# A Mamba scan over image tokens: the last token's decay is multiplied by C on GpSimd, the first token's u is replicated by TensorE, and the whole order is rewritten

## The chip, the cores and the metric

The kernel runs on one NeuronCore of a Trainium2 chip. The metric is the device time of one execution in microseconds (us), the median of several runs. The engines named below are TensorE (PE, with PEld for its weight loads), VectorE (DVE), ScalarE (ACT), GpSimd (POOL), and SyncE (SP), which here only issues DMAs.

## The reference, cut to what matters

Four layers run one after the other on an image of shape (2, 128, 128, 128), that is batch, channels, rows, columns. Layers 0 and 2 are alike and are the subject. Layer 1 is a window gate, and layer 3 a block of two 3x3 convolutions with batch norm. In layers 0 and 2, a 3x3 convolution is followed by a small Mamba model that sees the 128 values of each pixel as 8 tokens of 16 features:

```python
y = conv3x3(x, conv_w) + conv_b
seq = y.reshape(B*H*W, 8, 16)                 # 8 tokens of 16
xi, z = split(seq @ in_proj_w.T)              # 32 each
xc = silu(causal_conv_over_tokens(xi) + conv1d_b)
dt, Bm, Cm = split(xc @ x_proj_w.T, [1, 17])  # 1, 16, 16
dt = softplus(dt @ dt_proj_w.T + dt_proj_b)   # 32
dA  = exp(dt[..., None] * A)                  # 32 x 16
dBx = dt[..., None] * Bm[:, :, None, :] * xc[..., None]
for t in range(8):
    h = dA[t] * h + dBx[t]                    # 32 x 16 states, h = 0 at first
    ys[t] = sum(h * Cm[t], axis=-1)
out = ((ys + D * xc) * silu(z)) @ out_proj_w.T
```

Then come a group norm, a silu and the residual, which other parts of the kernel do.

## The kernel before, in words

**Tiles.** `_mamba` works on tiles of 4 image rows, that is 512 pixels in the free dimension. There are 64 tiles in each of the two layers, 128 in all. The 32 x 16 states of one token of one tile are an array of 128 partitions by 4 x 512 elements (`NJ = 4`, `NS = 512`), all in fp32.

**One token.** For token t, `decay` (L460, L469) makes the decay: 4 matmuls with 32 rows each fill two PSUM buffers named `set` (1024 elements each, one for each half `jp`), and ACT takes the exponential in place. `token` (L478, L479, L483) then does three DVE operations for each half: the decay times the old state, into PSUM; this product times C, into `r`; and the product plus the injected term, into the new state `h`. The part of y that comes from the token's own injection is not in `r`. It is computed apart as (sum of B C) times u, in `product`, `own` and `own_u`, with u = dt * xc. So y of token t needs only decay * old state * C here, and the last token needs no new state, so it has two operations for each half in place of three. `gather` (L498) sums `r` over the 16 states on PE, into a PSUM buffer `ys`.

**The injected term.** `store` writes u, and B with C, to DRAM. `load` (L441 to L446) reads them back for each of the tokens 0 to 6, replicated over the partitions: 1 MB into `ur` and 0.5 MB into `bcr` for each token. `inject` (L451) multiplies the two on GpSimd into `h`.

**Before the scan.** For each tile `conv` (9 taps), `turn` (a transpose), `project` (4), `silu`, `inout` (B, then C), `step` (dt, 2), `softplus`, `product`, `scaled` (u), `own` (2) and `own_u` prepare the inputs. Every one of the 12 matmul groups among them writes to the single PSUM buffer `one`, and the next group waits until ACT has copied it out. After the scan `through`, `gate`, `out`, `spread` and `keep` finish the tile.

**PSUM.** Three `set` buffers of two banks, one `ys` and one `one` fill the eight banks.

**The order.** Nothing is scheduled automatically. Each piece of work of tile k gets a place, k * `SPAN` + a constant, as in

```python
put(k, REP_AT + t, decay, t)
...
for _, _, f, args in sorted(todo, key=lambda x: x[:2]):
    f(*args)
```

All pieces of all tiles are emitted in the order of their places, and each engine runs its own instructions strictly in that order. A place isn't a time. It only says what is queued behind what. Pieces of three or four tiles are interleaved: while tile k is in its scan, tile k+1 is stored and loaded, and tile k+2 is projected. A buffer is handed out at the place of its tile's first writer, and that writer waits until the last reader of the earlier tile in this buffer is done.

Of the kernel before, what the change touches and what calls it, by code (L numbers as in the profile page):

```python
# [24 lines left out]
F32 = mybir.dt.float32  # L25
U8 = mybir.dt.uint8
AF = mybir.ActivationFunctionType
ALU = mybir.AluOpType
# [3 lines left out]
P = 128  # L32
NT, FT = 8, 16
DI, DS, DC = 32, 16, 4
NQ = 4
NJ = DI * DS // P
DJ = DI // NJ
# [4 lines left out]
NS = ROWS * P  # L42
# [229 lines left out]

SPAN = NT - 1
BAND_AT = -22.0
CONV_AT = (-12.75, -12.7, -11.6, -11.5, -11.35, -11.25, -11.2, -11.05, -10.85)
TURN_AT = -10.5
IN_AT = (-10.0, -9.75, -9.65, -9.05)
SILU_AT = -8.52  # L280
BC_AT = (-8.25, -7.45)
DT_AT = (-7.85, -6.7)
SOFTPLUS_AT = -5.62
PROD_AT = -6.85
OWN_AT = (-6.3, -5.8)
U_AT, OWN_U_AT = -5.0, -4.3
STORE_AT = -4.15
LOAD_AT, INJECT_AT = -3.7, -1.8
REP_AT = -1.2
SUM_AT = 0.35  # L290
D_AT = (1.25, 4.2)
V_AT = (3.79, 7.39)
OUT_AT, STATS_AT, KEEP_AT = 7.9, 12.5, 13.85


def _mamba(tc, src, w, con, dst, scratch, stats, H):


    nc = tc.nc
    ctx = ExitStack()  # L300
    bandp = ctx.enter_context(tc.tile_pool(name="bandp", bufs=2))
    seq = ctx.enter_context(tc.tile_pool(name="seq", bufs=2))
    tmp = ctx.enter_context(tc.tile_pool(name="tmp", bufs=2))
    st = ctx.enter_context(tc.tile_pool(name="st", bufs=1))
    ps_set = ctx.enter_context(tc.tile_pool(name="ps_set", bufs=3, space=PSUM))
# [5 lines left out]
    live = {}  # L311
    bands = {}

    def one():
        return ps_one.tile([P, NS], F32, tag="one", name="one")
# [5 lines left out]
    def conv(k, tap):  # L321

        if tap == 0:
            live[k] = {"py": one(), "band": bands[k * ROWS // BAND]}
        xb, py = live[k]["band"], live[k]["py"]
        r = (k * ROWS) % BAND
        kh, kw = divmod(tap, 3)
        nc.tensor.matmul(  # L328
            py.rearrange("p (r w) -> p r w", r=ROWS),
            lhsT=w["conv"][:, tap, :],  # L330
            rhs=xb[:, r + kh : r + kh + ROWS, kw : kw + P],
            start=(tap == 0),
            stop=(tap == 8),
        )
        if tap == 8:
            yc = live[k]["yc"] = tmp.tile([P, NS], F32, tag="yc", name="yc")
            nc.scalar.activation(yc, py, AF.Identity, bias=w["conv_b"])

    def turn(k):

        s = live[k]
        p = one()
        for r in range(ROWS):
            nc.tensor.transpose(p[:, r * P : (r + 1) * P], s["yc"][:, r * P : (r + 1) * P], con["ident"])
        s["y"] = tmp.tile([P, NS], F32, tag="y", name="y")
        nc.scalar.copy(s["y"], p)

    def project(k, i, g):
# [16 lines left out]
    def step(k, g):  # L365
        s = live[k]
        if g == 0:
            s["dt"] = seq.tile([P, 2, NS], F32, tag="dt", name="dt")
        p = one()
        nc.tensor.matmul(p, lhsT=w["dt"], rhs=s["xc"][:, g, :], start=True, stop=True)  # L370
        nc.scalar.activation(s["dt"][:, g, :], p, AF.Identity, bias=w["dt_b"])
# [10 lines left out]
    def store(k):  # L382

        s = live[k]
        su = s["su"] = scratch.tile([NT, DJ, NJ, NS], F32, tag="su", name="su")
        for g in range(2):
            for j in range(NJ):
                nc.sync.dma_start(
                    out=su[g * NQ : (g + 1) * NQ, :, j, :].rearrange("q e s -> (q e) s"),
                    in_=s["u"][j * NQ * DJ : (j + 1) * NQ * DJ, g, :],  # L390
                )

        sb = s["sb"] = scratch.tile([NT - 1, DS, 2, NS], F32, tag="sb", name="sb")
        for i, at in enumerate((0, DS)):
            nc.sync.dma_start(
                out=sb[:, :, i].rearrange("t n s -> (t n) s"), in_=s["bc"][at : at + P - DS, i, :]
            )
# [16 lines left out]

    def product(k):
        s = live[k]
        s["prod"] = tmp.tile([P, NS], F32, tag="prod", name="prod")
        nc.gpsimd.tensor_tensor(s["prod"], s["bc"][:, 0, :], s["bc"][:, 1, :], ALU.mult)  # L418

    def own(k, g):  # L420
# [8 lines left out]
    def own_u(k):  # L429
# [2 lines left out]
        nc.scalar.activation(s["xc"], s["xc"], AF.Copy, scale=w["d"])  # L432
        nc.gpsimd.tensor_tensor(s["t1"], s["t1"], s["xc"], ALU.add)

    def load(k, t):

        s = live[k]
        n = P - DS
        ur = s["ur", t] = st.tile([P, NJ, NS], F32, tag="ur", name="ur", bufs=3)
        u = s["su"][t]  # L440
        nc.sync.dma_start(out=ur[:n], in_=u[: DJ - 1].unsqueeze(0).to_broadcast([DS, DJ - 1, NJ, NS]))  # L441
        nc.sync.dma_start(out=ur[n:], in_=u[DJ - 1].unsqueeze(0).to_broadcast([DS, NJ, NS]))
        m = s["bc", t] = st.tile([P, 2, NS], F32, tag="bcr", name="bcr", bufs=5)
        b = s["sb"][t]
        nc.sync.dma_start(out=m[:n], in_=b.unsqueeze(1).to_broadcast([DS, DJ - 1, 2, NS]))
        nc.sync.dma_start(out=m[n:], in_=b)  # L446
# [6 lines left out]
    def decay(k, t):  # L453

        s = live[k]
        g, q = divmod(t, NQ)
        a = s["a", t] = [ps_set.tile([P, 2, NS], F32, tag="set", name="set") for _ in range(2)]
        for j in range(NJ):
            r = slice(j * NQ * DJ, (j + 1) * NQ * DJ)
            nc.tensor.matmul(  # L460
                a[j // 2][:, j % 2, :],
                lhsT=w["rep"][r, q, :],
                rhs=s["dt"][r, g, :],
                start=True,
                stop=True,
                tile_position=(r.start, 0),
            )
        for x in a:
            nc.scalar.activation(x, x, AF.Exp)  # L469

    def token(k, t, jp):

        s = live[k]
        if jp == 0:
            s["r", t] = st.tile([P, NJ, NS], F32, tag="r", name="r", bufs=2)
        pt = s["a", t][jp]
        js = slice(2 * jp, 2 * jp + 2)
        nc.vector.tensor_tensor(pt, pt, s["h", t - 1][:, js, :], ALU.mult)  # L478
        nc.vector.tensor_tensor(  # L479
            s["r", t][:, js, :], pt, s["bc", t - 1][:, 1].unsqueeze(1).to_broadcast([P, 2, NS]), ALU.mult  # L480
        )
        if t < NT - 1:
            nc.vector.tensor_tensor(s["h", t][:, js, :], pt, s["h", t][:, js, :], ALU.add)  # L483

    def through(k, g):

# [52 lines left out]
    def put(k, at, f, *args):  # L539
        todo.append((k * SPAN + at, len(todo), f, (k, *args)))  # L540

    for k in range(len(src) * ntile):
        if k * ROWS % BAND == 0:
            put(k, BAND_AT, band)
        for tap in range(9):
            put(k, CONV_AT[tap], conv, tap)
        put(k, TURN_AT, turn)
        for n in range(4):
            put(k, IN_AT[n], project, *divmod(n, 2))
        put(k, SILU_AT, silu)  # L550
        for i in range(2):
            put(k, BC_AT[i], inout, i)
        for g in range(2):
            put(k, DT_AT[g], step, g)
        put(k, SOFTPLUS_AT, softplus)
        put(k, PROD_AT, product)
        put(k, U_AT, scaled)
        for g in range(2):
            put(k, OWN_AT[g], own, g)
        put(k, OWN_U_AT, own_u)  # L560
        put(k, STORE_AT, store)
        for t in range(NT - 1):
            put(k, LOAD_AT + t, load, t)
            put(k, INJECT_AT + t, inject, t)
        for t in range(1, NT):
            put(k, REP_AT + t, decay, t)
            for jp in range(2):
                put(k, t - 1 + jp / 2, token, t, jp)
            put(k, SUM_AT + t, gather, t)
        for g in range(2):  # L570
            put(k, D_AT[g], through, g)
            put(k, V_AT[g], gate, g)
        put(k, OUT_AT, out)
        put(k, STATS_AT, spread)
        put(k, KEEP_AT, keep)
# [420 lines left out]
```

## Time and profile before

The median of 3 runs is 7862.33 us (7861.02 to 7884.91). The profiled execution has a span of 7860.9 us.

| | PE | DVE | ACT | POOL |
|---|---|---|---|---|
| busy us in the whole span | 6537.9 | 6831.1 | 4291.8 | 5521.1 |
| busy us in 600 us inside the first scan layer (1000 to 1600) | 510.7 | 574.3 | 363.8 | 473.8 |

A row of the profile's groups gives the line, the engine, the operation, output and input, the shapes and the count, then the busy time and the mean of one in ns, then the idle time of the engine just before these instructions and what ended it. In the timeline a row has the start and the duration in us, and in brackets the wait just before it with what ended it. "x8" on a PE row counts instructions: an fp32 matmul of 512 columns shows as two of them, so a convolution tap is x2 and one `decay` or `gather` is x8.

### The profile page before, as it was taken

To read this page: it belongs to the slowest core of one execution; us is meant where nothing else is said; L and a number is where in the kernel's file an instruction comes from. 1 tells how busy PE (TensorE), PEld (TensorE's weight loads), DVE (VectorE), ACT (ScalarE), POOL (GpSimd) and SP (SyncE) were. 2 spreads that over 40 slices of the span, in tenths; PEclk is the share of its full clock that TensorE was granted. 3 is DMA by queue.
4 is the path that set the end of the run, shared out by engine and by line. 5 is a ranking of instruction groups with operands and counts; after the bars stand their busy time and mean duration, and the time that the engine had idled before them with its cause. 6 is when DMAs were issued, how large, how long until landed. Compare 5 with 4: busy or idle time off the path is not lost. (4 is left out here: it accounts for less than half of the span.)

```text
span 7860.9 us, 86792 instructions
## 1 busy us (share of the span) xinstructions
PE 6537.9 (83%) x29412; PEld 2217.4 (28%) x29412; DVE 6831.1 (87%) x6360; ACT 4291.8 (55%) x4835; POOL 5521.1 (70%) x1810
## 2 busy tenths in 40 slices
PE   7888888888888888777888888888888888878893
PEld 2222222222222222253222222222222222223341
DVE  5999999999999999863999999999999999963454
ACT  5656666666666656482665665666656656621112
POOL 5777887777778777652777778787777777843330
PEclk8999999999999999866999999999999999979996
DMA  7999999999999999854999999999999999955204
GB/s 203 246 243 246 253 249 247 253 250 256 249 248 254 245 249 248 225 179 127 244 249 246 250 250 251 252 251 253 252 239 249 250 250 250 250 157 139 69 0 163
DMA packets 573435, 1765.42 MB, mean 225 GB/s; under 512 B 85536, under 2 KB 239680, under 8 KB 458176
## 3 DMA queue, kind: packets, MB, share of 16 engines
q1 hardware_dynamic: 530496, 1709.54, 84.0%
q10 hardware_dynamic: 42496, 50.34, 1.8%
q8 instruction: 234, 3.83, 0.2%
q14 instruction: 209, 1.71, 0.1%
HBM read 1549.82 MB, written 209.72 MB: 224 GB/s over the span
## 5 line engine op out<-in xcount | busy, mean ns | idle before, releaser
L451 POOL TENSOR_TENSOR h<-ur,bcr 128x2048 f32<-128x2048 f32 x896 | 4060.4, 4539 | 1193.2 <-DMA bcr<-sb 1006.0
L478 DVE TENSOR_TENSOR set<-set,h 128x1024 f32<-128x1024 f32 x1792 | 2193.0, 1224 | 301.6 <-ACT set L469 216.2
L479 DVE TENSOR_TENSOR r<-set,bcr 128x1024 f32<-128x1024 f32 x1792 | 2194.1, 1224 | 61.4
L469 ACT ACTIVATE set<-set 128x1024 f32<-128x1024 f32 x1792 | 1745.6, 1006 | 868.7 <-PE set L460 854.2
L483 DVE TENSOR_TENSOR h<-set,h 128x1024 f32<-128x1024 f32 x1536 | 1864.5, 1214 | 21.3 <-POOL h L451 21.2
L460 PE MATMUL set<-dt,rep 32*128 32x512 f32 x7168 | 1400.2, 674 | 96.8 <-DVE h L483 89.9
L498 PE MATMUL ys<-r,ct 128*32 128x512 f32 x7168 | 1166.1, 632 | 36.4 <-DVE r L479 36.0
L328 PE MATMUL one<-band,conv 128*128 128x512 f32 x2304 | 1085.5, 607 | 24.6 <-DMA band<-in_x_dram 12.2
L828 PE MATMUL m<-comb,u 128*128 128x512 f32 x1536 | 689.1, 610 | 88.5 <-DVE Y L842 53.2
L406 PE MATMUL one<-xc,keep 128*64 128x512 f32 x1024 | 324.6, 717 | 471.4 <-ACT xc L363 361.5
L460 PEld LDWEIGHTS set<-dt,rep 32*128 32x128 f32 x7168 | 405.2, 193 | 992.7 <-issue 466.2
L328 PEld LDWEIGHTS one<-band,conv 128*128 128x128 f32 x2304 | 408.2, 190 | 674.4 <-issue 599.2
L489 PE MATMUL ys<-t,ct 128*128 128x512 f32 x512 | 326.4, 724 | 252.4 <-DVE v L511 250.9
L357 ACT ACTIVATE xc<-one,keep 128x512 f32<-128x512 f32 x256 | 176.1, 688 | 519.5 <-PE one L355 514.7
L498 PEld LDWEIGHTS ys<-r,ct 128*32 128x32 f32 x7168 | 181.2, 111 | 928.5 <-issue 760.7
L828 PEld LDWEIGHTS m<-comb,u 128*128 128x128 f32 x1536 | 296.6, 195 | 480.3 <-issue 457.3
L426 PE MATMUL one<-prod,ct 128*128 128x512 f32 x512 | 290.3, 650 | 123.1 <-POOL prod L418 88.8
L380 POOL TENSOR_TENSOR u<-dt,xc 128x1024 f32<-128x1024 f32 x128 | 302.8, 2366 | 70.7 <-ACT dt L374 70.6
L355 PE MATMUL one<-y,w_in 128*128 128x512 f32 x512 | 343.5, 759 | 5.8 <-ACT xc L357 3.1
L469 ACT ACT_TABLE_LOAD x252 | 323.3, 1283 | 4.6
L370 PE MATMUL one<-xc,w_dt 128*128 128x512 f32 x512 | 313.5, 696 | 4.1 <-ACT bc L413 4.1
L427 ACT COPY t<-one 128x512 f32<-128x512 f32 x256 | 150.2, 587 | 301.4 <-PE one L426 301.4
(136 smaller groups left out, 5894.0 us busy)
## 6 DMA issues: line engine op xcount, KB each, us to landing
ur<-su SPq DMA_DIRECT2D x896, 896.0 KB, 11.5
bcr<-sb SPq DMA_DIRECT2D x896, 448.0 KB, 11.6
ur<-su SPq DMA_DIRECT2D x896, 128.0 KB, 11.1
su<-u SPq DMA_DIRECT2D x1024, 64.0 KB, 3.5
sb<-bc SPq DMA_DIRECT2D x256, 224.0 KB, 2.8
bcr<-sb SPq DMA_DIRECT2D x896, 64.0 KB, 10.9
y<-o SPq DMA_DIRECT2D x128, 256.0 KB, 9.2
band<-in_x_dram SPq DMA_DIRECT2D x28, 640.0 KB, 10.9
```

The costliest lines, as they stand in the source:

```text
L328: nc.tensor.matmul(py.rearrange("p (r w) -> p r w", r=ROWS), lhsT=w["conv"][:, tap, :], rhs=xb[:, r + kh : r + kh + ROWS, kw : kw + P], st ...
L355: nc.tensor.matmul(p, lhsT=w[("in", "z")[i]][:, g, :], rhs=s["y"], start=True, stop=True)
L406: nc.tensor.matmul(p[g * NQ * DS : (g + 1) * NQ * DS, :], lhsT=w[("xb", "xcm")[i]], rhs=s["xc"][:, g, :], start=True, stop=True,)
L451: nc.gpsimd.tensor_tensor(b, s["ur", t], s["bc", t][:, 0].unsqueeze(1).to_broadcast([P, NJ, NS]), ALU.mult)
L460: nc.tensor.matmul(a[j // 2][:, j % 2, :], lhsT=w["rep"][r, q, :], rhs=s["dt"][r, g, :], start=True, stop=True, tile_position=(r.start, 0),)
L469: nc.scalar.activation(x, x, AF.Exp)
L478: nc.vector.tensor_tensor(pt, pt, s["h", t - 1][:, js, :], ALU.mult)
L479: nc.vector.tensor_tensor(s["r", t][:, js, :], pt, s["bc", t - 1][:, 1].unsqueeze(1).to_broadcast([P, 2, NS]), ALU.mult)
L483: nc.vector.tensor_tensor(s["h", t][:, js, :], pt, s["h", t][:, js, :], ALU.add)
L489: nc.tensor.matmul(s["ys", g], lhsT=con["ident"], rhs=s["t1"][:, g, :], start=True, stop=False)
L498: nc.tensor.matmul(s["ys", g][a : a + NQ * DJ, :], lhsT=red[:, q, :], rhs=r[:, j, :], start=False, stop=(q == NQ - 1), tile_position=(0, a),)
L828: nc.tensor.matmul(m[:, i], lhsT=u[:, i, kw, :], rhs=v[:, i, :, kw : kw + P], start=(kw == 0), stop=(kw == 2),)
```

## The change

The change has four parts.

1. The last token. y of token 7 is (decay * C) times the state of token 6. The decay of token 7 is now written by its exponential to SBUF (`g`), a new piece `last` multiplies `g` by C on GpSimd (128 x 2048), and a new piece `end` does one DVE multiplication for each half in place of two. Because `end` reads the state of token 6 from PSUM, that token's addition writes in place there, and its two `set` buffers stay taken until `end`.
2. The first token. u of token 0 isn't stored and loaded. A new piece `first` replicates it with 4 matmuls of 32 rows against constants of -1 into two `set` buffers, and ACT copies them, times -1, into an `ur` buffer. `load` of token 0 brings only B and C. Token 7's u, which nobody read, isn't stored any more.
3. All places are new, and `SPAN` is 6.34 in place of 7. The decay of token 7 has a place of its own, `LAST_REP_AT`.
4. Buffers. `yc`, `y` and `prod` have one in place of two, `dt` has three in place of two, and `g` (8 KB in each partition) is new.

It is meant to take work off DVE and off the DMA engines.

```diff
-SPAN = NT - 1
+SPAN = 6.34
 BAND_AT = -22.0
-CONV_AT = (-12.75, -12.7, -11.6, -11.5, -11.35, -11.25, -11.2, -11.05, -10.85)
-TURN_AT = -10.5
-IN_AT = (-10.0, -9.75, -9.65, -9.05)
-SILU_AT = -8.52
-BC_AT = (-8.25, -7.45)
-DT_AT = (-7.85, -6.7)
-SOFTPLUS_AT = -5.62
-PROD_AT = -6.85
-OWN_AT = (-6.3, -5.8)
-U_AT, OWN_U_AT = -5.0, -4.3
-STORE_AT = -4.15
-LOAD_AT, INJECT_AT = -3.7, -1.8
-REP_AT = -1.2
-SUM_AT = 0.35
-D_AT = (1.25, 4.2)
-V_AT = (3.79, 7.39)
-OUT_AT, STATS_AT, KEEP_AT = 7.9, 12.5, 13.85
+CONV_AT = (-13.3, -13.15, -13.1, -13.1, -12.95, -12.95, -12.2, -12.15, -11.65)
+TURN_AT = -11.5
+IN_AT = (-11.45, -10.3, -9.55, -10.7)
+SILU_AT = -9.25
+BC_AT = (-9.1, -7.45)
+DT_AT = (-8.5, -8.0)
+SOFTPLUS_AT = -7.45
+PROD_AT = -7.35
+OWN_AT = (-7.3, -7.3)
+U_AT, OWN_U_AT = -7.35, -5.65
+STORE_AT = -4.75
+LOAD_AT, INJECT_AT = -3.3, -1.75
+REP_AT, LAST_REP_AT = -1.05, 3.45
+LAST_AT = 4.9
+PASS_AT = (5.7, 6.32)
+FIRST_AT = -4.85
+SUM_AT, LAST_SUM_AT = 0.25, 6.6
+D_AT = (1.2, 3.95)
+V_AT = (3.84, 6.75)
+OUT_AT, STATS_AT, KEEP_AT = 7.5, 13.0, 13.1
...
+    def first(k):
+
+        ur = room(k, 0)
+        for i, x in enumerate(four(con["neg"][:, :P], live[k]["u"][:, 0, :])):
+            nc.scalar.activation(ur[:, 2 * i : 2 * i + 2, :], x, AF.Copy, scale=-1.0)
...
+        a = s["a", t] = four(w["rep"][:, q, :], s["dt"][:, g, :])
+        if t < NT - 1:
+            for x in a:
+                nc.scalar.activation(x, x, AF.Exp)
+        else:
+            s["g"] = st.tile([P, NJ, NS], F32, tag="g", name="g")
+            for i, x in enumerate(a):
+                nc.scalar.activation(s["g"][:, 2 * i : 2 * i + 2, :], x, AF.Exp)
+
+    def last(k):
+
+        s = live[k]
+        c = s["bc", NT - 2][:, 1]
+        nc.gpsimd.tensor_tensor(s["g"], s["g"], c.unsqueeze(1).to_broadcast([P, NJ, NS]), ALU.mult)
...
-        if t < NT - 1:
-            nc.vector.tensor_tensor(s["h", t][:, js, :], pt, s["h", t][:, js, :], ALU.add)
+        h = s["h", t][:, js, :]
+        nc.vector.tensor_tensor(pt if t == NT - 2 else h, pt, h, ALU.add)
+
+    def end(k, jp):
...
+        nc.vector.tensor_tensor(s["r", NT - 1][:, js, :], s["a", NT - 2][jp], s["g"][:, js, :], ALU.mult)
```

## The prediction

> **What bounds the kernel now.** I read the page's slices first: in the two scan layers DVE and the DMA engines both stand at 9 tenths, GpSimd at 7 or 8.
>
> ```profile
> DVE  5999999999999999863999999999999999963454
> ...
> POOL 5777887777778777652777778787777777843330
> ...
> DMA  7999999999999999854999999999999999955204
> ```
>
> Then the windows, for one stretch inside layer 0 (length, then busy time and count of PE, PEld, DVE, ACT, POOL, then clock, DMA share, GB/s):
>
> ```profile
> 1000.00:1600.00 600.00, 510.73 (x2092) 159.57 (x2090) 574.28 (x508) 363.78 (x413) 473.82 (x139) 0.94 0.97 248
> ```
>
> Then the groups of that stretch:
>
> ```profile
> L451 POOL TENSOR_TENSOR h<-ur,bcr 128x2048 f32<-128x2048 f32 x84 | 380.8, 4540 | 122.5 <-DMA bcr<-sb 100.4 <-DVE set L478 8.4 <-DVE r L479 7.8
> ...
> L478 DVE TENSOR_TENSOR set<-set,h 128x1024 f32<-128x1024 f32 x165 | 202.0, 1224 | 18.3 <-ACT set L469 17.6
> ...
> L460 PE MATMUL set<-dt,rep 32*128 32x512 f32 x656 | 123.7, 676 | 5.4 <-DVE h L483 5.1
> ...
> L426 PE MATMUL one<-prod,ct 128*128 128x512 f32 x46 | 26.4, 656 | 13.9 <-POOL prod L418 11.9 <-ACT dt L371 2.0
> ```
>
> L478 comes 14 times a tile, so 600 us hold 165 / 14 = 11.79 tiles: 50.9 us a tile. In the timeline a half token on DVE (L478, L479, L483) is 3.53 us from start to start, a half of the last token 2.4, the three short ones 0.6 each: 12 x 3.53 + 2 x 2.4 + 1.8 = 49.0 us. DVE is the bound, with 2 us of waits a tile, nearly all for the decay's exponential. GpSimd waits for loads, hidden behind DVE.
>
> Last, the timeline, for the time of each link:
>
> ```profile
> 1242.93 1.14 PE L460 MATMUL set<-dt,rep 32*128 32x512 f32 x8
> ...
> 1244.11 1.93 ACT L469 ACTIVATE set<-set 128x1024 f32<-128x1024 f32 x2 [0.47 <-PE set L460]
> ...
> 1245.22 1.23 DVE L478 TENSOR_TENSOR set<-set,h 128x1024 f32<-128x1024 f32 x1 [0.26 <-ACT set L469]
> ...
> 1245.59 1.28 POOL L418 TENSOR_TENSOR prod<-bc 128x512 f32<-128x512 f32 x1
> ...
> 1246.92 1.13 PE L426 MATMUL one<-prod,ct 128*128 128x512 f32 x2 [0.80 <-POOL prod L418]
> ...
> 1248.09 0.59 ACT L427 COPY t<-one 128x512 f32<-128x512 f32 x1 [1.46 <-PE one L426]
> ...
> 1259.93 3.70 PE L328 MATMUL one<-band,conv 128*128 128x512 f32 x8
> ```
>
> A decay takes PE 1.1 us, its first exponential 1.0; `prod` 1.3, an `own` 1.1, its copy 0.6; a convolution tap 3.70 / 4 = 0.92; each link starts within 0.1 us of the one before. After long PE waits, products take twice as long:
>
> ```profile
> 1300.81 2.07 PE L426 MATMUL one<-prod,ct 128*128 128x512 f32 x2 [4.32 <-POOL prod L418]
> 1302.81 2.09 PE L460 MATMUL set<-dt,rep 32*128 32x512 f32 x8
> ```
>
> **What the Trainium skill says.** *GPSIMD Engine Reference*, section 3.1, gives 4497 ns for a two-input fp32 operation of 2048 elements; the trace has 4540. *ScalarE: Activation LUTs*, "What ACT_TABLE_LOAD costs", gives 1283 ns for a table load, as in the trace (1283), and 186 ns + 0.833 ns an element with immediate operands: my estimate for a copy of 1024 is 1.04 us. *TensorE: Matmul & The Clock Gate*, Part 1, says that PE falls to half rate after an idle window and needs a busy one to return; the 2.07 above against 1.13 agrees.
>
> **The change part by part.**
>
> *Removed from DVE:* 2 x 1.25 us a tile; `end` reads one operand from PSUM and one from SBUF like L479, and I give it L479's 1.15. DVE work: 12 x 3.53 + 2 x 1.15 + 1.8 = 46.5 us.
>
> *Removed from DMA:* of 12.6 MB a tile (248 GB/s x 50.9 us) the 1 MB load of token 0 and 0.13 MB of the store. 11.4 MB at 248 GB/s are 46.0 us.
>
> *Added to GpSimd:* `last`, 4.5 us: 473.8 / 11.79 = 40.2 becomes 44.7 us. Behind it are `prod` and u. *Added to PE:* `first`, 1.1 us, like a decay. *Added to ACT:* 2 x 1.04 us, giving 33 us of work. As sums, all of these stay below 46.5.
>
> *The single buffers* `yc`, `y`, `prod` cost nothing: each reader has finished long before the next writer's place. The third `dt` and the `g` buffer only remove waits.
>
> *The new order* decides. I sorted the places, assumed that a pool hands out the room free longest, and walked one tile with the durations above. Time 0 is the start of token 1 on DVE. Three waits come out.
>
> (a) `first` takes two of three `set` buffers behind token 2's first half, which ends at 11.8. PE 1.1, ACT copies to 14.8, the exponential of token 3's first half 14.9 to 15.9; DVE wants it at 15.3: 0.6 us.
>
> (b) The decays of tokens 7 and 5 stand behind `silu` on ACT. From 23.2: table and two silus 3.4, table 1.3, two exponentials 1.95, a copy 0.6, token 5's exponential 1.0: 31.5. DVE wants it at 30.7: 0.8 us.
>
> (c) Token 6's second `set` buffer is free when token 5's first half ends, at 35.0, and PE reaches this decay at 35.2. From there: decay 1.1; two exponentials to 38.3; the copy of C (`inout`) behind them 38.9; `prod` on GpSimd 40.2; `own` 0 41.4; its copy, behind the softplus, 42.05; `own` 1, which needs the same buffer `one`, 43.2; copy 43.85; and only then, because their places (5.72 to 6.07) lie before the next tile's first decay (6.29), six convolution taps, which need `one` too: 49.5; `gather` 50.6; the decay 51.7; its exponential 52.8. DVE ends its tile at 46.5 + 0.6 + 0.8 = 47.9 and waits 4.9 us. Before, the two `own` and the taps were spread between decays, and no decay stood behind the whole row.
>
> The sum is 46.5 + 0.6 + 0.8 + 4.9 = 52.8 us at PE's full rate. Queued behind are all the DVE work of the next tile and PE's remaining taps, so nothing wins it back. PE now idles about 2 us before token 7's second half and in pieces around the `own`; after waits of 1.9 to 4.3 us the trace shows up to 6 us at half rate. Unknown is how often this strikes: never gives 52.8; always, for the decay, B and decay behind the first wait (+2.0) and the two `own` (+1.9), 56.7. I take the two `own` in every second tile: 53.7 us. The sum is 7862 + 128 x (53.7 - 50.9) = 7862 + 358 = 8220 us.
>
> *Loads.* `first` holds one of three `ur` buffers from token 2 to token 0's injection, so loads 5 and 6 start only when the injection two before is done, with 4.5 us of GpSimd work to hide them. With 9 us to land (trace: 7.7 to 14.7) GpSimd waits about 4.6 us: its own round is 44.7 + 4.6 = 49.3, hidden under 53.7.
>
> **The rivals.**
>
> *Faster: DVE stays the bound.* If the walk has a wrong link and the waits stay 2 us, a tile takes 48.5: 7862 - 128 x 2.4 = 7555 us. For it: DVE is busy 96% of the stretch and loses 2.5 us; PE, ACT and GpSimd are below it as sums. Against it: (c).
>
> *Barely faster: GpSimd and its loads bound.* If PE passes `own` and taps earlier than I think, the round of 49.3 us with the late loads 5 and 6 remains, 7862 - 128 x 1.6 = 7657 us; at 11 us to land it is 51, no gain. For it: 100 us of waits for `bcr` in the stretch. Against it: it needs (c) to be wrong.
>
> *Much slower:* PE at half rate in every tile, 56.7 us: 7862 + 128 x 5.8 = 8604 us.
>
> **How the numbers follow.** Forecast 0.66, much slower 0.08, GpSimd and loads 0.14, DVE 0.12. The range must leave out at most 0.2: I drop the DVE case and the upper half of the much slower one, and a bit of the load case: 7650 to 8450. Within 0.3% lies the upper end of the load case and a (c) that is hidden: 0.06. Faster 0.2, slower 0.74.
>
> **What would show it.** Right: per tile about 53 to 54 us; L478 waits for the exponential some 6 us a tile, the longest before token 1 of each tile, directly behind six taps on PE; DVE busy about 87%, DMA share below 0.9; PE waits for `prod` at L426. Wrong: L478's waits still near 2 us a tile, or DVE waiting mostly at L483 for GpSimd, with GpSimd waiting for `ur` or `bcr`: then the loads bind.

## The result, and the profile after

The changed kernel takes 8484.02 us, the median of four runs (8473.08 to 8493.86), beside 7867.67 us for the kernel before on the same chip. The ratio is 1.0779 with a 95% interval of 1.0756 to 1.0802. That is 616 us more, or 4.8 us for each of the 128 tiles. The direction was forecast, the size was not: 8220 us was forecast, and 8450 was the upper end of the range.

The slices of the span in tenths, after:

```profile
DVE  4888888888888888863788888888888888883454
...
POOL 5877777788888888841788887888878778864331
...
DMA  5777777777777777753777777777777777765304
```

In the scan layers DVE and DMA both stood at 9 tenths before. Now neither DVE, nor GpSimd, nor DMA is full, and PE is busy for 516 of the 600 us below. So the lost time should lie in waits of one engine for another. The windows for the stretch that was shown of before (length, busy us and count of PE, PEld, DVE, ACT, POOL, then clock, DMA share, GB/s):

```profile
1000.00:1600.00 600.00, 515.89 (x2002) 166.08 (x2000) 501.76 (x445) 353.40 (x401) 474.63 (x136) 0.91 0.76 206
```

DVE lost 72.5 us of 574.3 in this stretch, and PE's granted clock fell from 0.94 to 0.91. The groups of the same stretch that answer to those of before:

```profile
L482 POOL TENSOR_TENSOR h<-ur,bcr 128x2048 f32<-128x2048 f32 x75 | 338.9, 4537 | 67.5 <-DMA bcr<-sb 42.6 <-DVE set L510 9.0 <-DVE r L511 8.9
L510 DVE TENSOR_TENSOR set<-set,h 128x1024 f32<-128x1024 f32 x131 | 160.5, 1225 | 93.8 <-ACT set L491 93.5
L449 PE MATMUL set<-dt,rep 32*128 32x512 f32 x606 | 144.1, 707 | 51.0 <-DVE h L515 41.3 <-ACT ur L463 7.2 <-ACT g L495 2.4
...
L431 PE MATMUL one<-prod,ct 128*128 128x512 f32 x42 | 27.6, 745 | 23.4 <-POOL prod L423 16.7 <-ACT t L432 6.8
```

L510 is called 12 times a tile now, so the stretch holds 131 / 12 = 10.9 tiles. L510 (L478 before) waits 93.8 us in place of 18.3, all but 0.3 us of it for the decay's exponential. The work that was taken from DVE is gone, and more time than that has come back as a wait. The wait before an exponential is PE's in the end: `decay` (L449) waits 51.0 us for a free `set` buffer in place of 5.4.

Where a tile differs from another is the quickest way to see what the wait is made of. Two tiles of this one profile, each from one multiplication L510 to the one twelve later:

```profile
303.31:356.31 53.00, 45.44 (x186) 14.58 (x185) 46.36 (x42) 32.52 (x38) 44.71 (x14) 0.97 0.80 215
915.36:975.16 59.80, 51.63 (x187) 16.63 (x187) 46.36 (x42) 32.61 (x38) 42.78 (x12) 0.84 0.68 184
```

The work is the same, with 46.36 us of DVE in both. The second tile takes 6.8 us longer at a clock of 0.84 in place of 0.97. (A clock of 0.5 in a record is PE's half rate, 1.0 its full rate, and a mean lies between.) The timeline shows where, first in the tile with the high clock (start, duration, and in brackets the wait before):

```profile
311.28 1.13 PE L431 MATMUL one<-prod,ct 128*128 128x512 f32 x2 [0.84 <-POOL prod L423]
...
313.08 1.12 PE L431 MATMUL one<-prod,ct 128*128 128x512 f32 x2 [0.68 <-ACT t L432]
...
314.88 5.42 PE L331 MATMUL one<-band,conv 128*128 128x512 f32 x12 [0.68 <-ACT t L432]
...
323.44 1.23 DVE L510 TENSOR_TENSOR set<-set,h 128x1024 f32<-128x1024 f32 x1 [3.66 <-ACT set L491]
```

and then in the other:

```profile
926.33 1.78 PE L431 MATMUL one<-prod,ct 128*128 128x512 f32 x2 [1.85 <-POOL prod L423]
...
928.78 2.07 PE L431 MATMUL one<-prod,ct 128*128 128x512 f32 x2 [0.68 <-ACT t L432]
...
931.53 8.07 PE L331 MATMUL one<-band,conv 128*128 128x512 f32 x12 [0.68 <-ACT t L432]
...
942.74 1.23 DVE L510 TENSOR_TENSOR set<-set,h 128x1024 f32<-128x1024 f32 x1 [9.79 <-ACT set L491]
```

This is the row of step (c), `prod`, own 0, copy, own 1, copy, six taps, then the next tile's first decay, and the wait of token 1 behind it. At full rate token 1 waits 3.66 us. With the two `own` and most of the taps at half rate it waits 9.79 us.

These two tiles are unlike most. Of 57 tiles in layer 0 only 12 have half rate on the `own`, by the clock records, and 50 have it further ahead, between decay 7 and token 5. From 1615 us on almost every tile of this layer is of one kind and takes 54.61 us. In the one from 1669.79 to 1724.40 half rate lasts from 1698.08 to 1704.91:

```profile
1696.50 1.13 PE L449 MATMUL set<-dt,rep 32*128 32x512 f32 x4 [2.40 <-DVE h L515]
...
1698.99 2.77 PE L449 MATMUL set<-dt,rep 32*128 32x512 f32 x8
...
1714.04 1.12 PE L431 MATMUL one<-prod,ct 128*128 128x512 f32 x2 [0.68 <-ACT t L432]
1715.84 5.42 PE L331 MATMUL one<-band,conv 128*128 128x512 f32 x12 [0.68 <-ACT t L432]
```

The first row is the second half of decay 7, after its wait for a `set` buffer, and the second is decay 5, 2.77 us in place of about 1.1. The `own` and the taps run at full rate here.

### The profile page after: what moved, and what is told of

It reads as the page before. It is cut to its first block, busy times and chain, and to the rows that moved or that the text cites. A ratio compares the mean times of both kernels' runs of the same rounds, so it can differ in the third digit from the quotient of the medians.

```text
span 8471.1 us, 87998 instructions
## 1 busy us (share of the span) xinstructions
PE 7059.4 (83%) x30436; PEld 2431.6 (29%) x30436; DVE 6536.1 (77%) x6104; ACT 4522.3 (53%) x5089; POOL 6086.8 (72%) x1938
## 5 line engine op out<-in xcount | busy, mean ns | idle before, releaser
L510 DVE TENSOR_TENSOR set<-set,h 128x1024 f32<-128x1024 f32 x1536 | 1881.8, 1225 | 1245.1 <-ACT set L491 1237.7
L491 ACT ACTIVATE set<-set 128x1024 f32<-128x1024 f32 x1536 | 1502.8, 1007 | 1538.4 <-PE set L449 1391.3
L449 PE MATMUL set<-dt,rep 32*128 32x512 f32 x7168 | 1683.7, 705 | 609.7 <-DVE h L515 510.7
L511 DVE TENSOR_TENSOR r<-set,bcr 128x1024 f32<-128x1024 f32 x1536 | 1880.1, 1224 | 52.7
L515 DVE TENSOR_TENSOR h<-set,h 128x1024 f32<-128x1024 f32 x1280 | 1551.5, 1212 | 0.0
L538 PE MATMUL ys<-r,ct 128*32 128x512 f32 x7168 | 1028.2, 621 | 23.7 <-DVE r L511 23.0
L449 PEld LDWEIGHTS set<-dt,rep 32*128 32x128 f32 x7168 | 491.6, 199 | 1755.6 <-issue 848.9
L501 POOL TENSOR_TENSOR g<-g,bcr 128x2048 f32<-128x2048 f32 x128 | 581.4, 4542 | 5.3 <-ACT g L495 5.3
L423 POOL TENSOR_TENSOR prod<-bc 128x512 f32<-128x512 f32 x128 | 162.1, 1266 | 486.6 <-ACT bc L418 486.6
L374 ACT ACTIVATE dt<-one,keep 128x512 f32<-128x512 f32 x256 | 176.1, 688 | 399.9 <-PE one L373 399.2
L438 POOL TENSOR_TENSOR t<-t,xc 128x1024 f32<-128x1024 f32 x128 | 301.0, 2351 | 90.1 <-ACT xc L437 66.9
L411 PE MATMUL one<-xc,keep 128*64 128x512 f32 x1024 | 342.7, 751 | 15.3 <-ACT xc L366 12.2
```

The costliest lines, as they stand in the source:

```text
L411: nc.tensor.matmul(p[g * NQ * DS : (g + 1) * NQ * DS, :], lhsT=w[("xb", "xcm")[i]], rhs=s["xc"][:, g, :], start=True, stop=True,)
L449: nc.tensor.matmul(a[j // 2][:, j % 2, :], lhsT=weights[r], rhs=moving[r], start=True, stop=True, tile_position=(r.start, 0),)
L501: nc.gpsimd.tensor_tensor(s["g"], s["g"], c.unsqueeze(1).to_broadcast([P, NJ, NS]), ALU.mult)
L511: nc.vector.tensor_tensor(s["r", t][:, js, :], pt, s["bc", t - 1][:, 1].unsqueeze(1).to_broadcast([P, 2, NS]), ALU.mult)
L515: nc.vector.tensor_tensor(pt if t == NT - 2 else h, pt, h, ALU.add)
L538: nc.tensor.matmul(s["ys", g][a : a + NQ * DJ, :], lhsT=red[:, q, :], rhs=r[:, j, :], start=False, stop=(q == NQ - 1), tile_position=(0, a),)
```

## The experiments

Each ratio below is that of the kernel to the kernel before on the same chip. "After" is the changed kernel.

**The row of step (c).** The six taps between own 1 and the next tile's first decay are moved directly behind that decay.

```diff
-CONV_AT = (-13.3, -13.15, -13.1, -13.1, -12.95, -12.95, -12.2, -12.15, -11.65)
+CONV_AT = (-12.72, -12.71, -12.7, -12.69, -12.68, -12.67, -12.2, -12.15, -11.65)
```

> Only the six taps move, from before the next tile's first decay to directly behind it on PE. Theory A (the taps in front of the decay are themselves the wait, as step (c) of the prediction says): the wait before token 1 loses the six taps, 5.5 us a tile, and falls from about 6 us to about 1; 8484 - 128 x 4.5 = about 7910 us. Theory B (PE's whole in-order row from the end of a tile's group of four tokens to the next tile is a ring; the taps have only one other place in it): the wait moves from token 1 to token 2, whose decay now stands behind the taps, and the time stays within 1% of 8484 us.

Measured: 8323.72 us, ratio 1.058 (1.0561 to 1.06). It is 160 us less than after, which is neither theory's number. The waits of the stretch 1000 to 1600 (total, times, longest):

```profile
DVE set L510 <- ACT set L491: 60.3, 25, 3.1
...
DVE v L551 <- PE ys L538: 24.8, 11, 2.3
```

The wait for the exponential falls from 93.5 to 60.3 us, but `gate` (L551), which waited for nothing in this stretch of after, now waits 24.8 us for `gather`, because the taps stand before it instead. The row was real, but most of what it cost only moved on.

**PE's clock.** Decay 7's first half (two products) is computed twice more while PE waits for the second half's `set` buffer. The repeated results are the same and nobody reads them in between.

```diff
-        for j in range(NJ):
+        for j in order:
...
-        a = s["a", t] = four(w["rep"][:, q, :], s["dt"][:, g, :])
+        a = s["a", t] = four(w["rep"][:, q, :], s["dt"][:, g, :], (0, 1, 0, 1, 0, 1, 2, 3) if t == NT - 1 else range(NJ))
```

> The products of the first half of token 7's decay are repeated twice (same values into the same buffer) while PE waits about 2.4 us for the second half's buffer. Theory C (the half rate after PE's waits is what the forecast took too small): the groups behind this wait, the decay's second half, B, token 5's decay and D, run at 1.1 us in place of about 2, token 5's wait falls by 1 to 2 us a tile, and the time falls by 130 to 250 us to 8230 to 8350 us. Rival (half rate there is hidden, or the half rate is not set by this wait): within 0.5% of 8484, or a little slower for the added 2.2 us of products.

Measured: 8409.91 us, ratio 1.0683 (1.066 to 1.0706). More work on PE makes the kernel 74 us faster, which speaks for the clock, but it lies outside both expectations, between them. A second try also filled the wait for `prod`:

```diff
         p = one()
+        for _ in range(1 * (g == 0)):
+            nc.tensor.matmul(p, lhsT=gsum[:, g, :], rhs=s["xc"][:, 0, :], start=True, stop=True)
         nc.tensor.matmul(p, lhsT=gsum[:, g, :], rhs=s["prod"], start=True, stop=True)
```

> The order of after, with products that nobody reads put on PE where it waits: decay 7's first half twice more before its second half (as in clock_fill), and one product into the buffer one ahead of the first own, while GpSimd makes prod. All results stay. This adds 3 us of work to PE in each tile. If the half rate behind these two waits costs what I think, a tile takes 52.5 us (all full) to 54.6 (half of it left): 8070 to 8340, faster than clock_fill's 8410. If the clock doesn't matter, the added work makes it slower than after, 8484 or more.

Measured: 8402.18 us, ratio 1.0674 (1.0655 to 1.0693), outside what was expected and no different from clock_fill within the intervals. The mean clock in 1000 to 1600 is 0.94 against after's 0.91, and still two 3.41 us stretches of nearly every tile are at half rate. They stand where after's usual tile has them, 28 us behind the start of token 1, and the tile takes the same 54.61 us. Filling the two waits took away after's tiles of other lengths, which are longer in the mean. It left this half rate in its place, though PE waits only 0.68 us for decay 7's second half there, in place of 2.40. So it isn't shown that this wait by itself brings the half rate.

**The first token's part.** u of token 0 is stored and loaded as before and `first` is left out, in after's order.

```diff
-        for a, b in ((1, NQ), (NQ, NT - 1)):
+        for a, b in ((0, NQ), (NQ, NT - 1)):
...
-        put(k, FIRST_AT, first)
```

> The changed kernel, but u of token 0 is stored and loaded as before, and first is left out. If first (its two set buffers, its copies on ACT, the ur buffer it holds) is part of the cause, the wait before token 3 (0.5 to 2.1 us) goes and the time falls by 60 to 270 us. If the ring from token 4 through own and taps to the next tile sets the time alone, what first costs is inside slack and the time stays within 0.7% of 8484 us, with the wait before token 1 longer by what token 3 no longer waits.

Measured: 8604.68 us, ratio 1.0906 (1.0846 to 1.0966), with runs from 8538.61 to 8682.04 us. By the ratios the kernel is about 100 us slower than after without `first`. So step (a) is not a cause that can be taken out by itself: PE has less to do, and is at half rate for 2477 us in its clock records (after 1686, before 1219).

**The work against the order.** The same work is put in the order of before: everything in before's places, the new pieces beside them. Then each of the two parts alone.

```diff
-SPAN = 6.34
+SPAN = 7
...
+REP_AT, LAST_REP_AT = -1.2, 4.5
 LAST_AT = 4.9
...
+PASS_AT = (6.0, 6.5)
+FIRST_AT = -3.0
+SUM_AT, LAST_SUM_AT = 0.35, 7.35
```

> The work of the change (both parts, its buffers) in the order of before: SPAN 7 and every place as it was, token 0's replication at -3.0, decay 7 at 4.5, its product with C at 4.9, the two last multiplications at 6.0 and 6.5. Theory O (the new order is what costs, the new work itself gains): faster than before, 7550 to 7750. Theory W (the new work costs in any order that was not made for it: the last tokens hold two set buffers longer, so PE waits and falls to half rate): slower than before, 8300 to 8650, that is 54.5 to 57 us a tile, with more half rate than before's 1219 us of the whole span.

> Only the last token's part in the order of before (token 0's u is stored and loaded as before; places as in old_places). Theory O: 2 us a tile less than before, about 7600. Theory W: 51 us a tile at PE's full rate and up to 55 with the half rate, so 7900 to 8400.

> Only the first token's part in the order of before (token 7 as before, its decay in its old place; the replication at -3.0). It adds a PE and an ACT piece on two set buffers and takes 1 MB of loads. Theory O: no change, 7800 to 7900. Theory W: 51 us a tile at full rate and up to 54 with the half rate, 7900 to 8250.

Measured: both parts 8804.4 us, ratio 1.1177 (1.1158 to 1.1196); the last token's part alone 8368.64, ratio 1.062 (1.0597 to 1.0642); the first token's part alone 8550.04, ratio 1.0853 (1.0835 to 1.0871). Theory W's direction holds, and its numbers are even exceeded by both parts together and by the first part. Its mechanism, that the last tokens hold `set` buffers longer, can't be what the first part alone costs. In before's order the new work costs 922 us, and the change's own places had won some 320 of them back. So beside before's order the new order is no loss. This is one placement of the new pieces, chosen by hand; others weren't tried. One group of both parts in the old order shows a price that was set too low, the replication of `first` on PE:

```profile
L449 PE MATMUL set<-u,ct 32*128 32x512 f32 x80 | 36.8, 1008 | 36.6 <-DVE h L515 22.4 <-ACT ur L463 11.6 <-POOL h L482 2.5
```

It waits 36.6 us, most of it for `set` buffers that the scan holds, and 60 of its 80 instructions run at half rate (a mean of 1008 ns an instruction, where after has 640).

**Is there an order in which the work pays?** A first order was found by walking through the queues with the durations of the traces at full rate.

> The same work and buffers as the changed kernel; all places chosen by walking the queues with the durations that the two traces show, so that no decay stands behind a long row: the own sums are apart, C and B come together and early, the last decay comes before the silus. If the order alone makes the loss, DVE's waits for the exponential fall from 9.7 us a tile to 1 to 2 and a tile takes 47 to 49 us: 7862 - 128 x 2.9 = 7490 us, between 7360 and 7620. If the new work makes the loss (last on GpSimd, first on PE and ACT, or the late loads 5 and 6), it stays above 7862 us.

Measured: 8086.23 us, ratio 1.0278 (1.0252 to 1.0303). It takes 398 us off after, but isn't what the walk promised, and stays above 7862 us. Half rate is still there, 1631 us in the clock records against after's 1686, so the 398 us are hardly the clock. DVE's wait for the exponential in the stretch 1000 to 1600 is 53.6 us in place of 93.5. The next orders came from replaying each engine's queue and its waits, with the half rate included.

> The work of the change with all places chosen anew, by replaying the engines' queues and waits with the durations of the traces and with the clock's behaviour seen in them[...]. The same replay gives before 50.5 us a tile at full rate and 52.5 with the clock (measured 50.9), after 51.3 and 54.6 to 55.7 (measured 55.8). Theory C (the work itself gains; waits on PE and the half rate that follows them took it back): 47.3 to 48.5 us a tile, 7400 to 7560, PE nearly always at full rate inside the scan layers, DVE busy for 95% there. Rival (the work costs something that no order avoids, loads or engines that share memory): 7862 or more.

Measured: 8805.92 us, ratio 1.119 (1.1165 to 1.1215), a plain miss. The replay had let the second half of `first` begin before its `set` buffer was free. The timeline shows the wait:

```profile
1264.29 2.07 PE L449 MATMUL set<-u,ct 32*128 32x512 f32 x4 [2.29 <-DVE h L515]
```

The work of before was retuned in the same way.

> The work of before with its places chosen anew by the same replay: it gives 50.3 us a tile against 50.5 to 52.5 for before's own places, since PE no longer falls to half rate. If new places alone bring the gain, this is as fast as retuned, 7400 to 7560. If the gain needs the new work, DVE's 49.0 us a tile stay and it is 7650 to 7820.

Measured: 7925.53 us, ratio 1.0064 (1.004 to 1.0087). These new places alone bring before nothing. They didn't do what the replay promised either, that PE no longer falls to half rate: its clock records have 1465 us of it, against before's 1219. Two more orders for the new work came from the mended replay.

> As retuned, from a mended replay: the first one let the second half of token 0's replication start before its set buffer was free. Decay 7 now stands between the decays of tokens 1 and 2. The mended replay gives 50.5 us a tile at full rate and 52.6 with the clock for before (measured 50.9), 52.4 and 54.6 for after (55.7), 54.3 and 61.4 for old_places (58.3), 51.6 and 55.0 for retuned (58.1), and 47.9 and 48.0 for this order. Theory C (waits on PE, and the half rate behind them, are what took the gain of the work): 47.5 to 49.5 us a tile, 7430 to 7680, PE at half rate for less than 3 us a tile. Rival (the new work can't be placed without such waits on the chip): 7862 or more.

> A second such order, with decay 7 between the decays of tokens 4 and 5 as in after: 48.4 us a tile in the replay, the same with and without the clock. Theory C: 48 to 50 us a tile, 7490 to 7750. Rival: 7862 or more.

Measured: retuned_2 takes 7760.34 us, ratio 0.9859 (0.9842 to 0.9877); retuned_3 takes 7971.36, ratio 1.0127 (1.0105 to 1.0149). Both are slower than expected, by 80 and 221 us beyond the upper ends, but retuned_2 is faster than both kernels, 1.4% below before. It does all the work of after, and only the places differ:

```diff
-CONV_AT = (-13.3, -13.15, -13.1, -13.1, -12.95, -12.95, -12.2, -12.15, -11.65)
-TURN_AT = -11.5
-IN_AT = (-11.45, -10.3, -9.55, -10.7)
-SILU_AT = -9.25
-BC_AT = (-9.1, -7.45)
-DT_AT = (-8.5, -8.0)
-SOFTPLUS_AT = -7.45
-PROD_AT = -7.35
-OWN_AT = (-7.3, -7.3)
-U_AT, OWN_U_AT = -7.35, -5.65
-STORE_AT = -4.75
-LOAD_AT, INJECT_AT = -3.3, -1.75
-REP_AT, LAST_REP_AT = -1.05, 3.45
-LAST_AT = 4.9
-PASS_AT = (5.7, 6.32)
-FIRST_AT = -4.85
-SUM_AT, LAST_SUM_AT = 0.25, 6.6
-D_AT = (1.2, 3.95)
-V_AT = (3.84, 6.75)
-OUT_AT, STATS_AT, KEEP_AT = 7.5, 13.0, 13.1
+CONV_AT = (-13.97, -13.96, -13.84, -13.72, -13.51, -13.41, -12.99, -12.94, -12.76)
+TURN_AT = -12.39
+IN_AT = (-11.75, -11.02, -10.35, -11.39)
+SILU_AT = -9.87
+BC_AT = (-8.97, -8.46)
+DT_AT = (-9.23, -8.91)
+SOFTPLUS_AT = -7.65
+PROD_AT = -8.46
+OWN_AT = (-7.66, -4.92)
+U_AT, OWN_U_AT = -6.83, -4.34
+STORE_AT = -5.57
+LOAD_AT, INJECT_AT = -3.61, -2.18
+REP_AT, LAST_REP_AT = -1.39, 0.17
+LAST_AT = 5.08
+PASS_AT = (5.46, 6.07)
+FIRST_AT = -5.03
+SUM_AT, LAST_SUM_AT = -0.04, 6.31
+D_AT = (0.69, 3.6)
+V_AT = (2.98, 6.59)
+OUT_AT, STATS_AT, KEEP_AT = 6.82, 13.0, 13.1
```

Its windows for the same stretch, and its L510:

```profile
1000.00:1600.00 600.00, 552.55 (x2262) 178.17 (x2260) 564.26 (x499) 398.61 (x452) 536.07 (x154) 1.00 0.88 232
```

```profile
L510 DVE TENSOR_TENSOR set<-set,h 128x1024 f32<-128x1024 f32 x146 | 178.7, 1224 | 26.5 <-ACT set L491 26.5
```

The clock is 1.00, DVE is busy 94% of the stretch, and L510 waits 26.5 us in place of 93.8. The stretch holds 12.2 tiles.

**One wait put back at a time.** In retuned_2 the two `own` stand apart (-7.66 and -4.92), and decay 7 stands between the decays of tokens 1 and 2 (0.17). Each of these two is put back alone.

```diff
-OWN_AT = (-7.66, -4.92)
+OWN_AT = (-7.66, -7.66)
```

> The order of retuned_2 with one place put back: the second own stands directly behind the first again, as in after (both at -7.66 in place of -7.66 and -4.92), so PE waits for ACT's copy of the first and the taps behind wait too. Nothing else differs. If the own row (step c) is a cause of its own, a tile takes 1.2 us more at full rate and up to 3.2 with the half rate behind it: 7910 to 8170. If only the place of decay 7 mattered, no change: 7750 to 7780.

```diff
-REP_AT, LAST_REP_AT = -1.39, 0.17
+REP_AT, LAST_REP_AT = -1.39, 3.45
```

> The order of retuned_2 with one other place put back: decay 7 at 3.45 as in after, between the decays of tokens 4 and 5 in place of those of tokens 1 and 2, so that its second half waits for a set buffer behind token 4. If PE's wait there and the half rate behind it cost what I think, a tile takes 2.7 to 4.1 us more: 8110 to 8290, with half rate back in every tile. If only the own row mattered, no change: 7750 to 7780.

Measured: 8192.98 us with the `own` together, ratio 1.0402 (1.0378 to 1.0426), and 8162.96 us with decay 7 late, ratio 1.0362 (1.0342 to 1.0382). That is 433 and 403 us more than retuned_2, or 3.4 and 3.1 us a tile. Either place alone undoes the gain and makes the kernel slower than before. In r2_own every tile of layer 0 has at least 6.8 us at half rate, so what the clock takes and the rest can't be told apart there. In r2_rep7 they can, since two neighbouring tiles differ in it (windows, columns as above):

```profile
352.49:402.25 49.76, 44.92 (x189) 14.40 (x188) 46.65 (x42) 32.61 (x38) 43.99 (x13) 1.00 0.83 223
402.25:455.00 52.75, 48.23 (x187) 14.83 (x187) 46.58 (x41) 33.20 (x38) 44.57 (x14) 0.90 0.81 223
```

On PE the two run alike, 50.05 us apart, from `out` (366.77 in the first) up to the product L373, after PE has waited 1.68 us for `silu`. The timeline of the first from there on:

```profile
387.92 1.13 PE L373 MATMUL one<-xc,w_dt 128*128 128x512 f32 x2 [1.68 <-ACT xc L366]
...
395.03 1.23 DVE L510 TENSOR_TENSOR set<-set,h 128x1024 f32<-128x1024 f32 x1 [0.99 <-ACT set L491]
```

and of the second:

```profile
437.97 1.72 PE L373 MATMUL one<-xc,w_dt 128*128 128x512 f32 x2 [1.68 <-ACT xc L366]
...
439.62 3.17 PE L449 MATMUL set<-dt,rep 32*128 32x512 f32 x8
...
447.93 1.23 DVE L510 TENSOR_TENSOR set<-set,h 128x1024 f32<-128x1024 f32 x1 [3.85 <-ACT set L491]
```

From `out` on, instructions, order and waits are the same up to here. In the second tile the clock falls at 438.37; decay 7 (L449), the product behind it and decay 5 run at half rate, and token 5 waits 3.85 us in place of 0.99. That is nearly all of the 3.0 us between the tiles. The tile at full rate takes 49.76 us, only 0.4 more than the 49.4 of retuned_2's usual tile. It is not a lone one: from token 1 to token 1, the four tiles of layer 0 that have no half rate take 50.05 or 50.06 us each, and the mean is 52.6. So the late decay 7 costs little by itself, about 0.6 us by these four. It puts two decays behind one another where PE has just waited, and most of the price, some 2.5 of 3.2 us a tile, goes with the half rate that strikes them.

## Why the prediction was wrong

*What held.* DVE's work: 46.5 us forecast, 46.36 measured in a tile. The three waits are in the three places forecast, before tokens 3, 5 and the next tile's token 1, and all are for the exponential (2.11, 2.88 and 7.15 us in the tile from 1218.88 to 1277.69). Their sum at full rate was forecast as 6.3 us, and the tile of 53.00 us at a clock of 0.97 has 53.00 - 46.36 = 6.64 us without DVE work. That the sum is so close is in part luck: the wait before token 1 was forecast as 4.9 us and is 3.66, the one before token 5 as 0.8 and is 1.63, and 0.45 us before token 4 weren't forecast. So 52.8 us at PE's full rate was right within about 1 us: 53.00 in this tile, which still has one window at half rate, and 51.8 by the fit below. The loads stayed hidden, as forecast: GpSimd waits 42.6 us for `bcr` in the stretch, 4 us a tile, and DVE's wait is for ACT.

*What failed* is the last term of the sum, "I take the two `own` in every second tile: 53.7 us", which adds 0.9 us for PE's half rate. A mean tile in 1000 to 1600 takes 600 x 12 / 131 = 55.0 us, and by the whole result 50.9 + 4.8 = 55.7. Measured from the forecast's own 52.8, the term is 2.2 to 2.9 us and not 0.9. By the fit below it is larger still, 8.5 us at half rate x 0.41 = 3.5 us, and a full-rate sum 1 us too long hid a part of it.

The term was mis-sized because the half rate strikes far more often, and mostly in another place. Of 57 tiles of layer 0, 12 have it on the `own`, which is one in five and not every second. 50 have it behind decay 7's wait, and this the forecast had put in the unlikely case only. So in the tile at 1247.21, after a wait of 2.40 us, decay 7's second half takes 1.81 us, B 1.98 and the decay behind them 2.09. What the like is worth shows in r2_rep7, 3.0 us between two tiles of one kernel. And where half rate does strike the `own`, it reaches farther down the row: the six taps behind them take 7.64 or 8.07 us in place of 5.42, and the forecast had priced them at full rate in every case. The rival "much slower" at 56.7 us had priced the common event, at every tile, together with the rarer one, and got 0.08.

The prediction also took 2.07 us against 1.13 as agreeing with an idle window. The time is doubled, but in the window before the half rate PE was busy for 0.97 of 3.41 us (see the last section).

*A part that was not seen as one.* The 50.9 us of before contain half rate as well. In its own trace a tile at a clock of 1.00 takes 48.94 us, and its mean is near 50.6 in layer 0:

```profile
303.18:352.12 48.94, 42.04 (x179) 13.54 (x178) 48.46 (x45) 30.86 (x35) 36.85 (x12) 1.00 0.97 247
```

Fitted over 57 tiles of before and 52 of after in layer 0 (tile time against the time at half rate, from the clock records), a tile takes 49.1 us + 0.28 x the half-rate time before, and 51.8 + 0.41 x after, with means of 5.0 and 8.5 us at half rate. By these fits some 2.6 of the 4.7 us that layer 0 lost are waits at full rate, and 2.1 are the clock. The split is an estimate from the spread within two profiles. No run has after's order at full rate throughout, since filling the waits didn't remove the half rate.

*Why the gain of the work didn't come.* DVE's 2.6 us a tile were gained: 46.4 in place of 49.0. They were lost on PE, which was no bound by its sum. The new work takes `set` buffers in new places and makes PE wait, DVE then waits for the exponential behind PE, and half rate lengthens both. That most of this loss is set by the order and not by the work itself, retuned_2 shows: the same work in other places takes 7760 us.

It doesn't show that the work gains. At a clock of 1.00 a tile of retuned_2 takes 49.4 us, and one of before 48.94 (49.1 in the mean of its 16 such tiles in layer 0). DVE's 2.6 us are lost again, 2.2 of them before L510, mostly at tokens 2 and 3. What retuned_2 has over before's mean of 50.6 us is the half rate, which it nearly avoids and before doesn't. Whether the work of before would be as fast in an order without half rate is not tested: before_retuned was meant to be such an order and isn't.

## What to carry to other kernels

When a change takes work from the engine that is full, ask which engine its new order lets wait in the middle of the chain, and price what that engine does just after the wait at the rate that its clock then grants, in both the old and the new kernel. If the tiles of one profile differ in time with the same busy time, compare their granted clocks before any other explanation. And judge the work and the order apart. Put the new work in the old order before calling either of them the cause, since here the order that looked guilty had saved some 320 us. Compare tiles at the full clock of both kernels before crediting the work with a gain: here the best order found for it was still not shorter than the old kernel's own full-rate tile.

## What the runs showed of the hardware

**The half rate needs no idle window.** The Trainium skill (*TensorE: Matmul & The Clock Gate*, Part 1) says that PE falls to half rate after an idle window of 3413 ns, with windows that run freely. The length agrees with the clock records here: stretches of half rate last 3.41 us or a multiple. "Idle" doesn't agree. Windows of this length, of before

```profile
1295.52:1298.93 3.41, 0.97 (x8) 0.06 (x4) 2.25 (x2) 1.20 (x2) 3.41 (x1) 1.00 1.02 246
1298.93:1302.34 3.41, 1.53 (x2) 0.50 (x2) 2.78 (x3) 0.00 (x0) 2.46 (x3) 0.50 1.00 222
```

and of after

```profile
1261.18:1264.59 3.41, 1.37 (x5) 0.54 (x4) 3.38 (x4) 2.92 (x3) 2.25 (x2) 1.00 0.90 255
1264.59:1268.00 3.41, 2.74 (x4) 0.65 (x4) 3.38 (x4) 1.71 (x2) 3.41 (x2) 0.50 0.63 192
1268.00:1271.42 3.42, 3.42 (x6) 1.33 (x5) 2.53 (x3) 0.16 (x1) 3.42 (x2) 0.50 0.79 240
```

show PE (the first busy time) at work for 0.97 of 3.41 us and for 1.37, and the next window is at half rate each time. In the first, PE's wait of 4.32 us begins inside the window; in the second there are only waits of 1.36 and 0.68 us, with products before, between and behind them. The window with 2.74 us of work (80%) is followed by another at half rate, and the full one behind it by full rate.

How busy PE has to be isn't settled by this. In layer 0 of before, 75 of 77 falls follow a window at most 0.44 busy. In after's, 59 of 77 follow a fuller one, up to 0.75. Full rate came back only behind windows at least 0.9 busy, in both traces, but 45 of after's half-rate windows in which PE was busy throughout were followed by half rate again. (Busy times of PE are modelled by the profile.) The replays had set half rate behind a window less than about half busy, and full rate behind one over 90% busy. Before's trace is near to that and after's is not, which may be why the replays were too hopeful.

**Tile times lock to the clock's window.** A tile of old_last:

```profile
1213.34:1267.95 54.61, 46.91 (x182) 15.73 (x178) 46.27 (x42) 30.94 (x36) 44.35 (x14) 0.88 0.88 235
```

54.61 us are 16 windows of 3.413 us. In layer 0, 54 of 56 tiles of old_last take this time to 0.1 us. So do 33 of 55 of after, and nearly all of clock_fill and of fill_two. In such a row of tiles the half rate falls in the same place of each. It may be that it sets the tile's length, and the length where the next one falls. This may be why filling waits bought so little, and why fill_two, with a product more on PE, is the same as clock_fill. It wasn't tested by itself.
